# A two-layer adaptive feed-forward kernel: layer 1's order of instructions planned anew, layer 0's last sums regrouped, last outputs on two queues

## The chip, the cores and the metric

The kernel runs on one core of a Trainium2 chip. The core has a matrix engine (TensorE, PE in the profile; its weight loads are shown apart as PEld), a vector engine (VectorE, DVE), a scalar engine (ScalarE, ACT), GpSimd (POOL) and SyncE (SP), which here mostly issues DMAs. Each engine works through its own instructions in order, and semaphores make it wait for the others. The metric is the device time of one execution, in microseconds (us). Before the change the median of three runs was 423.62 us (423.48 to 424.63).

## The reference, cut to what matters

The input x has 8 batches of 128 tokens (1024 tokens) of 512 features. Each of two layers computes a condition from x, feeds it to a gated feed-forward network, and adds the result to x:

```python
# layer 0: base projection plus a gated mixture of 8 low-rank experts (top 2), then 4-bit weights
c = x @ W.T + 2.0 * sum_e gate[e] * (x @ A[e].T) @ B[e].T
x = x + (silu(c @ Wgate0) * (c @ Wup0)) @ Wdown0       # 1376 inner, weights dequantised by groups of 128

# layer 1: one 512x512 weight per batch, chosen by an index; RMS norm; then float32 weights
c = x @ weight[adapter_id].T
n = c * rsqrt(mean(c*c) + 1e-5) * ln_w
x = x + (silu(n @ gate_w.T) * (n @ up_w.T)) @ down_w.T  # 1792 inner
```

All of it is float32, and the result must be as exact as float32.

## The kernel before, in words

Activations are kept transposed: features on the 128 partitions (four chunks, `KC`), tokens along the free axis in two blocks `tb` of 512. `xT` is the residual x, updated in place and written out at the end.

**Splitting.** Most products are made with a faster matmul type. An operand is split into a high part (made on ScalarE, `high_of`, line 1069), a low part and a scaled difference (VectorE, `low_of` line 1072, `difference_of` line 1075). A sum takes high and low products ("H") and difference products ("D") into one PSUM bank, and between the two the bank is multiplied by a constant in place (`rescale`, done on ScalarE or VectorE through `scaled`, lines 1199 and 1201). TensorE therefore waits, at each change from H to D or back, for one engine to have gone over a bank.

**Layer 0** (`by_groups_of_scales`, the usual path) is written out by hand inside one `tc.manual_schedule` region: in it TensorE, VectorE and ScalarE issue in the order in which the code emits. Small splitting and dequantising jobs are put in queues for ScalarE and VectorE (`queue`), and are emitted when an estimate of the engines' load lets them (`spent` calls `pump`) or when `flush(name)` forces them out. The eleven chunks j of the inner dimension run in pairs (`gate_up_pair`, matmuls on line 659, `rescale` lines 299 and 301), and the down products (line 707) by blocks of chunks. The tail is `last_chunk_and_down`: gate and up of chunk 10 (96 wide), with the down products of chunks 8, 9 and 10 between them. `first(m)` multiplies chunk 8 into the sum of output chunk m, and needs the high part (first half of its matmuls) and the low part (second half, DVE line 313) of `h8`; `second(m)` adds chunk 9, after a rescale of the sum; last comes chunk 10, and `down_final` (line 719) adds the finished sum to `xT`. The last loop is over tb outside and m inside: all four m of the first 512 tokens, then all four of the other 512. Two of the four sums, m = 2 and 3, take the PSUM of `gate` and `up`, and so must wait until the silu (line 675) and the product h (line 678) have read these. Meanwhile `queue_first_weights` splits, for layer 1's chunk 0, two of four groups of weights: group 0 (high, low, difference, then sums of weights) and group 2.

**Layer 1** is not written by hand. `Plan` holds tasks, each with its engine or engines, an estimated duration, dependencies, a priority `key`, and the buffers it takes and gives. `Plan.run` plays them through at build time: of the tasks whose dependencies are done, the one with the lowest key begins on a free engine, and the instructions are emitted in that order (again inside a `manual_schedule` region of its own). A finished task is seen at once by tasks that can only run on the same engine, and by others after `SEEN[engine]` (0.22 us after PE, 0.16 us after ACT or DVE). Keys come from constants: `STEP`, `LEAD` (how far before a chunk its weights are split), `AT` (places of the 29 steps of a chunk), `DOWN_LAG`, `DOWN_LEAD`, `SOON` (how early the rows' norms come), `SOONER` and `FILL` (the first three chunks), `WAYS` (which rescales may go to either engine and which to ScalarE alone), and others.

The tasks: eight rows (batches, order `ROWS1`): `adapt` (float32 products with the batch's weight, line 1261, 8 matmuls a row), then square, root, reciprocal, nx, turn (transposes, line 1302), norm, and splits of the row's forms (lines 1226 to 1232). The first row reads the first 128 tokens of all four m of `xT`. Then 14 chunks: gate and up for a pair of token halves through seven products of combined operands (matmuls on line 1446, snapshots on 1480 and 1484, products h on 1534), 42 matmuls a chunk. The down products (line 1585) come in five blocks; a block's eight sums (tb, m) take H, a rescale, D, and then `done` (line 1624, VectorE) adds them to `xT`. In the last block each `done` also issues the DMA of that piece of `xT` to the output (line 1626), all nine on SyncE's queue; the last sum is done in two halves.

Of the kernel before, what the change touches and what calls it, by code (L numbers as in the profile page):

```python
# [14 lines left out]
F32 = mybir.dt.float32  # L15
# [8 lines left out]
P = 128  # L24
# [33 lines left out]
PASS = 0.2267  # L58
SEEN = {"pe": 0.22, "act": 0.16, "dve": 0.16, "pool": 6.0, "sp": 3.5}
ANY_ORDER = {"bank", "snap"}  # L60
LATE = {"snap": 6, "sl": 2, "h3": 4, "wd": 2, "d": 3}
STEP = 1.41
LEAD = 8.17
DOWN_LAG = 10.29
DOWN_LEAD = 12.73
SOON = 6.82
OWN = 7.12
MIXED = 0.75
X22_AT = 4.98
H_AT = 10.2  # L70
D_STEP = 5.98
R_AT = -7.84
DD_AT = 4.69
DONE_AT = 6.56
WAYS = [0, 0, 0, 0, 0, 1, 1, 1, 0, 0]
SOONER = [[10, 10, 10, 10], [30, 0, -1.09, 0], [40, 12.63, 0, 0]]
FILL = [2.15, 4.34, 16.57]
XS_ONLY = (0, 1, 2, 16, 17, 18)
WEIGHTS_AT = [0.55, 1.73, 1.0, 2.54]
AT = [0.0, -1.2, -2.2, 1.9, 0.51, 2.5, 2.78, 3.97, 3.64, 3.1, 4.78, 6.47, 5.56, 6.5, 7.0, 7.5, 1.66, 2.64, 5.26, 4.46, 3.66, 4.42, 4.78, 5.36, 8.09, 7.2, 6.62, 7.62, 8.03]  # L80
# [48 lines left out]
class Plan:  # L129
# [12 lines left out]
    def run(self):  # L142
# [10 lines left out]
        def begin(t, engine, us):  # L153
            nonlocal n
            waiting.remove(t)
            for k, who in t.takes:
                queue[k].remove(t)
                self.place[k, who] = self.slots[k].pop(0)
            t.on = engine
            if engine is not None:  # L160
                begun[engine] = now + us
                n += 1
                heapq.heappush(events, (now + us, n, None))
            own = [s for s in t.then if list(s.engines) == [engine]]
            for some, at in ((own, now + us), (None, now + us + SEEN.get(engine, 0.0))):
                n += 1
                heapq.heappush(events, (at, n, (t, some)))
            if t.fn is not None:
                t.fn(engine)
# [13 lines left out]
        while left:  # L183
# [5 lines left out]
            while events and events[0][0] <= now + 1e-6:  # L189
# [3 lines left out]
                t, some = t  # L193
                if some is None:
                    left -= 1
                    some = [s for s in t.then if list(s.engines) != [t.on]]
# [17 lines left out]
def network_in(ctx, tc, a, out, by_groups, flag, again):  # L214
# [25 lines left out]
    cp = cond_stack.enter_context(tc.tile_pool(name="cond", bufs=1, side="right"))  # L240

# [331 lines left out]
    def by_groups_of_scales():  # L573
# [129 lines left out]
        def down_product(ps, m, k, first, tbs=range(NTB)):  # L703
            n = CH0[k]
            for i in range(2):
# [9 lines left out]
            spent(2 * len(tbs))  # L715
# [19 lines left out]
        def last_chunk_and_down():  # L735
# [7 lines left out]
            def gate_up(c):  # L743
                for half, ps in enumerate(gu):
# [7 lines left out]
            def first(m):  # L752
                down_product(sums[m], m, j - 2, True)
                rescale(sums[m], ratio_d[:, m, j - 2 : j - 1])
# [7 lines left out]
            first(0)  # L762
            gate_up(1)
            first(1)
            gate_up(2)
            flush(f"h{j - 1}")
            second(0)
            gate_up(3)
# [13 lines left out]
            for tb in range(NTB):  # L782
                for m in range(KC):
                    down_product(sums[m], m, j, False, range(tb, tb + 1))
                    down_final(xT[:, m, tb * TB : (tb + 1) * TB], m, sums[m][:, tb], group)
# [31 lines left out]
        with tc.manual_schedule(engines={EngineType.PE, EngineType.DVE, EngineType.Activation}):  # L817

            nc.scalar.activation(root, eps, AF.Exp)
            exp0 = experts(0)  # L820
            x_high(0)
            x_low(0)
            x_scaled(0)
            exp1 = experts(1)
            for m in range(2):
                w_high(m)
            hg0 = gated(0, rows_of(exp0))
            for m in range(2, KC):
                w_high(m)
            kept = cp.tile([P, 2, 2 * (E + E * R)], F32, name="kept")  # L830
            nc.scalar.copy(kept, exp1[:, :, : 2 * (E + E * R)])
            x_high(1)
            scale_bT()
            pairs0, base0 = base_sums()
            for m in range(KC):
                base_products(base0, 0, m, 0)
            hgT0 = turned(hg0, exp0[:, 0, :])
            for m in range(KC):
                w_low(m)
                base_products(base0, 0, m, 1)  # L840
            x_low(1)
            x_scaled(1)
            for ps in pairs0:
                rescale_base(ps)
            pairs1, base1 = base_sums()
            for i in range(2):
                for m in range(KC):
                    base_products(base1, 1, m, i)
            x_diff(0)
            for m in range(KC):  # L850
                w_diff(m)
                base_products(base0, 0, m, 2)
            hg1 = gated(1, [kept[:, i].rearrange("p (b n) -> p b n", b=2) for i in range(2)])
            for ps in pairs1:
                rescale_base(ps)
            x_diff(1)
            queue_zeros(0, 4, "zeros")
            for j in range(4):
                queue_weights(j, f"w{j}")
            flush("w0")  # L860
            for i in range(2):
                for m in range(2 * i, 2 * i + 2):
                    low_rank(base0, hgT0, m)
                split_condition(0, pairs0[i], i)
            ratios(ratio, sc)
            flush("w1")
            ratios(ratio_d, scd)
            for m in range(2):
                base_products(base1, 1, m, 2)
            hgT1 = turned(hg1, base0[0])  # L870
            base_products(base1, 1, 2, 2)
            for i in range(2):
                for m in range(2 * i, 2 * i + 2):
                    if m == KC - 2:
                        base_products(base1, 1, KC - 1, 2)
                    low_rank(base1, hgT1, m)
                split_condition(1, pairs1[i], i)
                if i == 0:
                    for _ in range(2):
                        run("dve", 0)  # L880
            cond_stack.close()
            open_rw()
            pools["w1"] = w1_stack.enter_context(tc.tile_pool(name="w1", bufs=1, side="right"))
            hp = h_stack.enter_context(tc.tile_pool(name="h0", bufs=1, side="right"))
            load_down(*BLOCKS0[0])
            for pair0 in PAIRS0[2:4]:
                load_qw(*pair0)

            def dequantise(pair0, zeros=None):
                if zeros is not None:  # L890
                    queue_zeros(*zeros, "zeros")
                for j in range(*pair0):
                    queue_weights(j, f"w{j}")

            def ready(pair0):
                for j in range(*pair0):
                    flush(f"w{j}")

            load["act"], load["dve"] = clock[0] + 1.0, clock[0] + 2.0

            queue_down(*BLOCKS0[0], "d0", at=clock[0] + 7.0)
            gate_up_pair(0, 1)
            ready(PAIRS0[1])
            dequantise(PAIRS0[2], (4, 8))
            gate_up_pair(2, 3)
            flush("d0")
# [892 lines left out]
```

## Time and profile before

| | us |
|---|---|
| median of three runs | 423.62 |
| the profiled execution, its own time | 423.74 |
| its span, first to last instruction | 421.9 |
| PE busy | 411.8 |
| DVE busy | 373.0 |
| ACT busy | 307.0 |
| layer 0's last product starts / layer 1's first adapt product starts | 165.25 / 165.57 |
| last matmul ends | 415.28 |

The span is what the profile's views are about; 1.8 us of the execution's own time lie outside it. The mean granted TensorE clock is 0.995 over the span. In a timeline row the columns are: start, duration, engine, line, operation, output<-inputs, shape, how many were merged, and in brackets the idle time of that engine before it and who ended it. A matmul's duration contains its pipeline; what counts is the distance from one start to the next. In the chain of waits, 64 down products back to back (line 707, from 72.32 us) take 14.51 us, 0.2267 us each; ten adapt products (from 180.92 us) take 4.29 us, 0.429 us each; four transposes 0.44 us.

### The profile page before, as it was taken

How to read it: one execution, taken by the hardware profiler on the slowest of the kernel's cores; microseconds unless marked ns; L12 is line 12 of the kernel's file. 1: busy time of each engine (PE TensorE's matmuls, PEld its weight loads, DVE VectorE, ACT ScalarE, POOL GpSimd, SP SyncE). 2: the span in 40 equal slices, each digit the busy share in tenths (PEclk: the TensorE clock that was granted, in tenths of full speed). 3: DMA queues.
4: the chain of work that ended last, by engine and by line, in shares of the span. 5: the costliest groups of instructions: out<-in, count | busy, mean ns of one | idle time of the engine just before them, and what ended most of it. 6: DMA issues, size and time to landing. Idle time of an engine off the chain costs nothing.

```text
span 421.9 us, 5201 instructions
## 1 busy us (share of the span) xinstructions
PE 411.8 (98%) x1771; PEld 314.9 (75%) x1771; DVE 373.0 (88%) x678; ACT 307.0 (73%) x503; POOL 27.1 (6%) x34
## 2 busy tenths in 40 slices
PE   8999999999999999999999999999999999999993
PEld 8885778888888765445676777788778877887772
DVE  4799979997998689989999999988998899979963
ACT  5833798868796765668998787658975797669651
POOL 1000200000000300320011011011011001000000
PEclk9999999999999999999999999999999999999997
DMA  8931811010010720870163035033323134000014
GB/s 271 394 144 36 233 56 44 11 53 2 0 62 2 278 46 18 329 239 2 58 181 62 0 87 138 0 87 88 113 50 89 62 75 114 0 3 1 24 51 155
DMA packets 16913, 38.59 MB, mean 91 GB/s; under 512 B 1904, under 2 KB 8432, under 8 KB 15856
## 3 DMA queue, kind: packets, MB, share of 16 engines
q1 hardware_dynamic: 11344, 25.09, 17.8%
q0 software_dynamic: 4960, 12.06, 11.5%
q10 hardware_dynamic: 576, 1.05, 0.6%
q8 instruction: 15, 0.25, 0.2%
q14 instruction: 18, 0.15, 0.1%
HBM read 36.10 MB, written 2.10 MB: 91 GB/s over the span
## 4 chain that ended last, share of the span: by engine, by line
PE 85%; DVE 8%; ACT 4%; issue 1%; ACTq 0%; DVEq 0%
PE bank L1446 27%; PE bank L1585 17%; PE gate L659 9%; PE up L659 9%; PE down L707 8%; PE base L510 5%; PE bank L1261 5%; PE experts L413 2%; PE base L536 2%; DVE w L1072 1%; DVE xT L719 1%; DVE w L1075 1%; PE idle L366 1%; PE bank L1302 1%; DVE snap L1534 1%
## 5 line engine op out<-in xcount | busy, mean ns | idle before, releaser
L1199 ACT ACTIVATE bank<-bank 128x512 f32<-128x512 f32 x129 | 73.3, 584 | 31.9 <-PE bank L1446 17.6
L1585 PE MATMUL bank<-h,d 128*128 128x512 f32 x240 | 66.5, 391 | 0.2
L1585 PEld LDWEIGHTS bank<-h,d 128*128 128x128 f32 x240 | 44.8, 188 | 10.6 <-DVE snap L1480 0.6
L659 PE MATMUL gate<-a,dq 128*128 128x512 f32 (+1 forms) x176 | 47.8, 393 | 0.1
L659 PE MATMUL up<-a,dq 128*128 128x512 f32 (+1 forms) x176 | 47.4, 391 | 0.0
L1446 PE MATMUL bank<-xs,w 128*128 128x512 f32 x168 | 46.0, 396 | 0.8 <-ACT bank L1199 0.8
L1446 PE MATMUL bank<-a,w 128*128 128x512 f32 x168 | 45.2, 394 | 0.2 <-ACT snap L1199 0.2
L707 PE MATMUL down<-h,wd 128*128 128x512 f32 (+1 forms) x176 | 42.6, 395 | 0.6 <-DVE h L313 0.4
L707 PEld LDWEIGHTS down<-h,wd 128*128 128x128 f32 (+1 forms) x176 | 32.4, 188 | 10.0 <-DVE xT L719 1.3
L659 PEld LDWEIGHTS gate<-a,dq 128*128 128x128 f32 (+1 forms) x176 | 32.5, 185 | 8.5 <-ACT sl L675 0.6
L659 PEld LDWEIGHTS up<-a,dq 128*128 128x128 f32 (+1 forms) x176 | 32.4, 185 | 7.9 <-DVE a L791 0.4
L1446 PEld LDWEIGHTS bank<-xs,w 128*128 128x128 f32 x168 | 31.1, 188 | 9.1 <-ACT bank L1199 1.6
L1446 PEld LDWEIGHTS bank<-a,w 128*128 128x128 f32 x168 | 30.7, 188 | 9.0 <-ACT snap L1199 2.2
L1075 DVE SCALAR_TENSOR_TENSOR w<-w 128x512 fp32r<-128x512 f32 x50 | 34.5, 690 | 2.1
L299 ACT ACTIVATE gate<-gate,ratio 128x1024 f32<-128x1024 f32 (+1 forms) x24 | 26.1, 1086 | 10.7 <-PE gate L659 10.7
L1480 DVE SCALAR_TENSOR_TENSOR snap<-bank,snap 128x512 f32<-128x512 f32 x42 | 28.6, 684 | 4.9 <-ACT wz L1069 4.8
L1072 DVE TENSOR_TENSOR w<-raw,w 128x512 fp32r<-128x512 f32 x42 | 28.7, 684 | 3.1 <-ACT w L1069 3.1
L1062 POOL DMA_DIRECT2D raw<-in_wgu x14 | 17.4, 1246 | 208.2 <-PE gate L659 45.6
L1624 DVE SCALAR_TENSOR_TENSOR xT<-bank,xT 128x512 f32<-128x512 f32 (+1 forms) x41 | 27.4, 672 | 3.0 <-PE bank L1585 2.6
L1585 PE MATMUL bank<-w,d 128*128 128x512 f32 x96 | 29.4, 391 | 0.0
L1261 PE MATMUL bank<-w,xT 128*128 128x512 f32 x64 | 29.2, 596 | 0.0
L1199 ACT ACTIVATE snap<-bank 128x512 f32<-128x512 f32 x41 | 24.2, 593 | 5.9 <-PE bank L1446 5.8
(169 smaller groups left out, 736.9 us busy)
## 6 DMA issues: line engine op xcount, KB each, us to landing
raw<-in_wgu SPq DMA_DIRECT2D x14, 640.0 KB, 4.0
raw<-in_wgu POOLq DMA_DIRECT2D x14, 256.0 KB, 4.4
wd<-in_wd SPq DMA_DIRECT2D x14, 256.0 KB, 2.7
qw<-in_qw_gu SPq DMA_DIRECT2D x5, 512.0 KB, 4.7
xT<-in_xT SPq DMA_DIRECT2D x2, 1024.0 KB, 12.2
out<-xT SPq DMA_DIRECT2D x7, 256.0 KB, 2.0
xb<-in_xb ACTq DMA_DIRECT2D x4, 256.0 KB, 5.2
xb<-in_xb SPq DMA_DIRECT2D x4, 256.0 KB, 5.2
```

The costliest lines, as they stand in the source:

```text
L299: nc.scalar.activation(ps, ps, AF.Copy, scale=by)
L510: nc.tensor.matmul(base[m], lhsT=wT3[i][:, m, c * P : (c + 1) * P], rhs=x_parts(tb)[i][:, c, :], start=(i == 0 and c == 0), stop=(i == 1 a ...
L659: nc.tensor.matmul(ps, lhsT=dqs[j][:, c, half, :], rhs=a3[i][:, c, tb * TB : (tb + 1) * TB], start=(c == 0 and i == 0), stop=(i == 1), ski ...
L707: nc.tensor.matmul(ps[:, tb], lhsT=wds[k][:n, m * P : (m + 1) * P], rhs=h2[k][i][:, tb], start=(first and i == 0), stop=(i == 1), skip_gro ...
L1072: nc.vector.tensor_tensor(lo, raw, hi.bitcast(F32), ALU.subtract)
L1075: nc.vector.scalar_tensor_tensor(di, lo.bitcast(F32), -1.0 / EPS, hi.bitcast(F32), ALU.mult, ALU.add)
L1199: nc.scalar.activation(out_, in_, AF.Copy, scale=by)
L1261: nc.tensor.matmul(of("bank", "ad", b), lhsT=xT[:, c, b * T : (b + 1) * T], rhs=of("w1", b)[:, c * D : (c + 1) * D], start=(c == 0), stop= ...
L1446: nc.tensor.matmul(ps, lhsT=w[:, i, n, c * P : (c + 1) * P], rhs=x[i][:, c0 + c], start=(first and i == which[0] and c == 0), stop=True, s ...
L1480: nc.vector.scalar_tensor_tensor(x, of("bank", j, bank_), by, x, ALU.mult, ALU.add)
L1585: nc.tensor.matmul(of("bank", *who), lhsT=of("d", j)[:, i, m * P : (m + 1) * P], rhs=h_tile(j, tb)[:, i], start=(i == 0 and j == j0), stop ...
L1624: nc.vector.scalar_tensor_tensor(x, of("bank", *who)[:, q * w : (q + 1) * w], -EPS, x, ALU.mult, ALU.add)
```

## The change

1. `Plan.run`: a finished task is now seen by waiting tasks that have `"pe"` among their engines `WEIGHTS` = 0.11 us later than by others (unless that task can only run on the same engine). The buffers it gives come free as before.
2. Most constants of layer 1's keys have new values, two of the `WAYS` (snapshot v to ScalarE alone, snapshot u3 to either), and the assumed times at which VectorE and ScalarE become free for layer 1 (2.6 and 0.0 us for 2.0 and 0.3).
3. Group 2 of layer 1's chunk 0 is no longer split by `queue_first_weights` at the end of layer 0, but by tasks of the plan, as the other chunks' groups are.
4. `last_chunk_and_down`: `first(0)` is cut in two: its high half comes before `gate_up(1)` and its low half after it; the split of chunk 9's h is forced out between them. `second(0)` and the last gate and up products are interleaved by halves.
5. The last loop of layer 0 goes by m: both token blocks of one m (four matmuls), then one `down_final` over 1024 columns; for the last m two of 512.
6. The two `manual_schedule` regions become one, closed after the plan has run.
7. In the last block, the DMAs of sum 6 and of the first half of sum 7 are issued by ScalarE, the others by SyncE as before.

```diff
+WEIGHTS = 0.11
-STEP = 1.41
-LEAD = 8.17
-DOWN_LAG = 10.29
-DOWN_LEAD = 12.73
-SOON = 6.82
+STEP = 1.36
+LEAD = 7.63
+DOWN_LAG = 13.45
+DOWN_LEAD = 13.99
+SOON = 8.12
...
-WAYS = [0, 0, 0, 0, 0, 1, 1, 1, 0, 0]
-SOONER = [[10, 10, 10, 10], [30, 0, -1.09, 0], [40, 12.63, 0, 0]]
-FILL = [2.15, 4.34, 16.57]
+WAYS = [0, 0, 0, 1, 0, 0, 1, 1, 0, 0]
+SOONER = [[10, 10, 10, 10], [30, 0.2, -1.09, 3.36], [47.42, 20.05, 7.42, 7.42]]
+FILL = [2.92, 7.12, 17.38]
...
-            own = [s for s in t.then if list(s.engines) == [engine]]
-            for some, at in ((own, now + us), (None, now + us + SEEN.get(engine, 0.0))):
+            some = {True: [], "pe": [], False: []}
+            for s in t.then:
+                some[True if list(s.engines) == [engine] else "pe" if "pe" in s.engines else False].append(s)
+            seen = now + us + SEEN.get(engine, 0.0)
+            for some, at, last in (
+                (some[True], now + us, False), (some[False], seen, True), (some["pe"], seen + WEIGHTS, False)
+            ):
...
             gate_up(0)
-            first(0)
+            first(0, range(1))
+            flush(f"h{j - 1}")
             gate_up(1)
+            first(0, range(1, 2))
             first(1)
             gate_up(2)
             flush(f"h{j - 1}")
-            second(0)
-            gate_up(3)
+            second(0, range(1))
+            gate_up(KC - 1, range(1))
+            second(0, range(1, NTB))
+            gate_up(KC - 1, range(1, 2))
             queue_split(f"h{j}", h, h2[j])
...
-            for tb in range(NTB):
-                for m in range(KC):
-                    down_product(sums[m], m, j, False, range(tb, tb + 1))
-                    down_final(xT[:, m, tb * TB : (tb + 1) * TB], m, sums[m][:, tb], group)
+            for m in range(KC):
+                down_product(sums[m], m, j, False)
+                if m < KC - 1:
+                    down_final(xT[:, m, :].rearrange("p (b t) -> p b t", b=2), m, sums[m], group)
+                else:
+                    for tb in range(NTB):
+                        down_final(xT[:, m, tb * TB : (tb + 1) * TB], m, sums[m][:, tb], group)
...
-    plan = Plan(slots, {"dve": 2.0, "act": 0.3})
+    plan = Plan(slots, {"dve": 2.6, "act": 0.0})
...
-            if j == 0 and g in (0, 2):
+            if j == 0 and g == 0:
...
-                        nc.sync.dma_start(out=out[m * P : (m + 1) * P, cols], in_=x)
+                        by = nc.scalar if i >= NTB * KC - 2 and q == 0 else nc.sync
+                        by.dma_start(out=out[m * P : (m + 1) * P, cols], in_=x)
```

## The prediction

> **What bounds the kernel now.** First the page's busy times, then the stretches of the layers one by one.
>
> ```profile
> PE 411.8 (98%) x1771; PEld 314.9 (75%) x1771; DVE 373.0 (88%) x678; ACT 307.0 (73%) x503; POOL 27.1 (6%) x34
> ...
> 142.00:165.60 23.60, 22.95 (x94) 15.53 (x92) 19.50 (x31) 18.07 (x23) 0.00 (x0) 1.00 0.32 101
> 165.60:182.00 16.40, 16.05 (x48) 7.43 (x48) 15.24 (x32) 7.51 (x19) 5.88 (x5) 1.00 0.74 246
> 182.00:196.00 14.00, 14.00 (x43) 6.62 (x42) 12.38 (x28) 11.01 (x28) 1.04 (x1) 1.00 0.41 152
> 196.00:206.00 10.00, 9.17 (x40) 6.42 (x41) 9.25 (x21) 9.35 (x24) 0.00 (x0) 1.00 0.01 2
> 206.00:236.00 30.00, 29.83 (x125) 22.14 (x124) 28.95 (x51) 26.90 (x54) 2.57 (x2) 1.00 0.40 106
> 236.00:266.00 30.00, 29.75 (x127) 23.02 (x126) 28.76 (x49) 23.16 (x44) 2.40 (x2) 1.00 0.33 79
> 298.00:402.00 104.00, 104.00 (x450) 82.78 (x449) 95.24 (x162) 79.31 (x150) 4.81 (x4) 1.00 0.21 54
> ```
>
> TensorE is the bound, but its busy time hides small waits, since a matmul's 0.39 us overlaps the next. The counts show them: at 0.2267 us a matmul, 206 to 236 has 125 x 0.2267 = 28.3 of 30 us (1.7 lost), 236 to 266 has 28.8 (1.2 lost), 298 to 402 has 102.0 of 104 (2.0 lost). In 196 to 206, counted by kind (0.2267, adapt 0.429, transpose 0.11), some 8.3 of 10 us (1.7 lost), and from 165.6 to 196 about 0.8. So layer 1 loses 7.4 us, most of it in its first hundred; in 196 to 206 ScalarE (9.35 of 10) and VectorE (9.25) are nearly full.
>
> Where single waits lie, from the timeline:
>
> ```profile
> 147.66 0.73 PE L707 MATMUL down<-h,wd 128*128 128x512 f32 x2 [0.43 <-DVE h L313]
> ...
> 157.48 2.12 PEld L707 LDWEIGHTS down<-h,wd 128*128 128x128 f32 x10 [0.62 <-DVE h L678]
> ...
> 162.14 5.36 DVE L719 SCALAR_TENSOR_TENSOR xT<-down,small,xT 128x512 f32<-128x512 f32 x8
> ...
> 164.91 0.30 PEld L707 LDWEIGHTS down<-h,wd 96*128 96x128 f32 x2 [0.36 <-DVE xT L719]
> 165.57 0.30 PEld L1261 LDWEIGHTS bank<-w,xT 128*128 128x128 f32 x2 [0.36 <-DVE xT L719]
> ...
> 172.20 0.66 PE L1302 MATMUL bank<-ident,nx 128*128 128x128 f32 x4 [0.35 <-ACT nx L1199]
> ...
> 205.62 1.20 PE L1446 MATMUL bank<-xs,w 128*128 128x512 f32 x4 [0.75 <-ACT bank L1199]
> 206.65 1.07 PE L1446 MATMUL bank<-a,w 128*128 128x512 f32 x4
> ```
>
> Four matmuls take 1.20 us after a wait and 1.07 without one: besides the wait, about 0.11 us goes on a weight load that nothing covers (start to start 0.34 instead of 0.227). The end, SyncE's issues and one of the landings:
>
> ```profile
> 413.96 2.12 DVE L1624 SCALAR_TENSOR_TENSOR xT<-bank,xT 128x512 f32<-128x512 f32 x4 [0.90 <-PE bank L1585]
> ...
> 415.36 1.17 SPq L1626 DMA_DIRECT2D out<-xT  x1
> ...
> 417.17 0.87 SPq L1626 DMA_DIRECT2D out<-xT  x1
> ...
> DMA to landing us min/median/max: 2.5/2.5/2.5
> ```
>
> VectorE is done at 416.08; the last transfer is issued 1.1 us later, as its queue is busy with the two before it (1.17 and 0.45 us for an issue that takes 0.33 when the queue is free), and lands at 419.7; 2.2 us of closing follow.
>
> **The change, part by part.**
>
> *Layer 0's tail, gate and up.* The wait before 147.66 is for the low half of `h8`. Cutting `first(0)` lets eight matmuls (1.8 us) go between: 0.6 of waiting and 0.1 of weight load go. Late next is `gate_up(1)`: it moves up to 147.05, its gate sum leaves ScalarE's rescale at 147.07 and its up sum at 148.07, where the matmuls arrive at about 147.96, so 0.3 comes back. Forcing out the split of `h9` puts VectorE's low part (1.2) ahead of the rescales; a rescale on ScalarE from 149.05 (when the high part ends there) takes 1.1 and meets `gate_up(2)` at 150.4; behind the low part on VectorE it would end at 151.6 and cost 1.2. Net -0.3, bounds -0.7 to +0.8. The halving of the last gate and up ends the gate sum 0.45 sooner, so the silu (1.1) and h (1.27) that free the PSUM for `first(3)` end sooner by at most that; the wait before 157.48 falls from 0.5 to some 0.3: -0.2 (0 to -0.45).
>
> *Sums by chunk.* TensorE starts chunk 10's sixteen down matmuls at 161.09 and adapt at 165.57: 4.48 us, against 16 x 0.2267 = 3.63. The rest is that the second token block's product of each m waits for the first's `down_final` (0.67 us each, eight in 5.36). With four matmuls a sum nothing reads a sum still being made: -0.85. What it costs: VectorE's first addition starts after four matmuls, not two, at about 162.2 (without group 2's low part, 0.69 us, which stood in front of it at 161.53), and from 1.2 us each (the 1024-wide rows of VectorE) sums 0 to 2 are in `xT` at 163.4, 164.65 and 165.9, sum 3's first half at 166.6. Row 0's adapt pairs, from 164.72 at 0.86 us each, need them at 164.72, 165.6, 166.4 and 167.3: covered, by 0.5 for the third. If that cover goes, each 0.1 beyond it costs 0.1. Bounds 0 to -0.95.
>
> *Group 2 of chunk 0* moves 0.63 us of ScalarE and 1.37 of VectorE from layer 0's end into layer 1; VectorE's 0.69 in front of the additions is off the path now, and ScalarE has an idle 5.1 us before its first square (169.31) to take it. I take 0; if it lands after 193, where ScalarE runs without a break to 205.6, it costs up to 2.0.
>
> *One region.* The order across the boundary shows no gap now (0.32 us from the last product to adapt, explained by VectorE). No instruction is added: 0, bounds -0.3 to +0.3.
>
> *Layer 1's order.* Every matmul is still there, 924 of them on lines 1446 and 1585; what can change is the 7.4 us lost. Two pieces have visible causes. Row 0's turn waited 0.5 beyond need since its reciprocal stood behind VectorE's splits until 171.26 (root ready 170.32); larger `SOON` puts rows' norms ahead. And each wait behind a rescale pays the 0.11 that the planner had not counted; some 25 places in layer 1 do, 2.8 us. A planner that counts it prefers a task already loaded. I take a third of the loss, -2.4, since 196 to 266 is as much bound by ScalarE and VectorE as by order; bounds -5.0 (the stretch before 266 as dense as 298 to 402) and +2.0 (as much again lost in the first hundred us as a third of what is lost).
>
> [...]
>
> *The outputs.* ScalarE is idle from 413.86. Sum 6 is issued there at 415.36, its first half of 7 after it; SyncE is free at 415.0 and can issue the last half at 416.1 instead of 417.17. Landing after 2.5 gives 418.6; after 3.6 (the longest among these) 419.7, no gain. I take -0.8, bounds 0 to -1.1.
>
> [...]
>
> Sum: 423.74 - 0.3 - 0.2 - 0.85 - 2.4 - 0.8 = 419.2; the profiled execution is 0.12 above the median, so **419.1**.
>
> **Rivals.** (a) The new order loses as much as the old: VectorE has only 0.75 to 1.2 us idle in each of the three stretches from 196 to 266, and TensorE that arrives 1.35 earlier finds the same busy engines. For it: the full 196 to 206; against: ScalarE's idle 9 us in 165.6 to 182. Then 423.62 - 1.35 - 0.8 = 421.5, or, if the earlier start is also lost there, 422.8. (b) Slower: the splits moved into layer 1 and the chunk-2 splits that `SOONER` calls 7.4 us earlier stand on VectorE and ScalarE ahead of the rows' forms, so that chunk 0's first sums come late. Price: 2.0 for group 2 and three more splits' high and low (3 x 1.3 = 3.9) at worst, with the 1.35 of layer 0 lost as well: 423.62 - 0.8 + 2.0 to 5.9, or 424.8 to 428.7. It decides when more than 0.8 us of such work stands ahead between 193 and 206. For it: ScalarE's unbroken run there; against: the early idle time. (c) The planner counts 0.11 on every hand-over, though most are hidden; if it so leaves gaps that a real TensorE doesn't, nothing is lost (the engine goes on when it can), so no price of its own.
>
> **How the numbers follow.** The forecast, with layer 1 better by 1 to 5 us: 0.55, its own range 416 to 421. Rival (a): 0.27, split evenly between 421.5 and about 422.8. Rival (b): 0.16. Better than 415.5: 0.02. A measurement of this kernel tells 0.3% (1.3 us, so 422.35 and 424.9) from no change. Faster: 0.55 + 0.02 + 0.15 = 0.72; same 0.13; slower 0.15. The range, 415.5 to 424.9, leaves out some 0.17.
>
> **What would show it.** Right: no wait on line 313 in the middle of the tail; line 719 with three 1024-wide additions; adapt 3.6 us after chunk 10's first down product; the first hundred us of layer 1 with more matmuls per stretch; the last issue within 0.2 us of VectorE's end. Wrong: adapt waiting for additions to `xT`, TensorE waiting for rescales longer between 190 and 206, or SyncE's last issue landing no sooner.

## The result and the profile after

The changed kernel takes 425.33 us (median of seven executions, 424.94 to 426.46) against 424.14 us for the kernel before beside it: a ratio of 1.0034, with a 95% interval of 1.0025 to 1.0044. It is slower by about 1.4 us. One execution of all those below, in the run without the forced split of `h9`, was slow throughout (691.3 us at a mean granted clock of 0.559) and is left out there. The prediction had 419.1 with a range up to 424.9, so it missed in size and in sign.

The two profiled executions (span 421.9 before, 423.3 after) are first cut at three events that both have. "Lost" is the time from the first adapt product to the start of layer 1's last matmul, less 240.27 us: the work between them at the pitches given above (0.2267, 0.429 and 0.11 us, and 0.025 for two very short ones).

| stage, us | before | after | difference | predicted |
|---|---|---|---|---|
| start to the first gate product of layer 0 | 41.88 | 42.69 | +0.81 | 0 |
| from there to the first adapt product | 123.69 | 123.42 | -0.27 | -1.35 |
| from there to the start of the last matmul | 249.32 | 250.65 | +1.33 | -2.4 |
| of that, lost | 9.05 | 10.39 | +1.33 | |
| from there to the end of the span | 7.05 | 6.55 | -0.5 | -0.8 |

The first row is not the change: the instructions there are the same, and over the fourteen profiles of this study that start lay anywhere between 41.6 and 42.8, always 29.7 us after TensorE's first product. What moves that first product (11.9 to 13.1) was not followed. The page's busy times hide all of it, as they did before:

```profile
PE 409.2 (97%) x1771; PEld 316.7 (75%) x1771; DVE 374.4 (88%) x677; ACT 306.8 (72%) x504; POOL 27.6 (7%) x34
```

The stretches (columns: window, length, then busy time and number of instructions of PE, PEld, DVE, ACT and POOL, granted clock, DMA share, GB/s) show where layer 1 won and lost:

```profile
165.60:182.00 16.40, 16.40 (x51) 7.85 (x51) 16.02 (x33) 8.87 (x24) 5.95 (x5) 1.00 0.78 264
196.00:206.00 10.00, 9.86 (x44) 7.33 (x45) 9.24 (x21) 9.38 (x25) 0.00 (x0) 1.00 0.18 54
206.00:236.00 30.00, 26.10 (x113) 20.28 (x112) 27.48 (x49) 24.55 (x49) 2.53 (x2) 1.00 0.31 80
236.00:266.00 30.00, 29.12 (x125) 22.70 (x124) 29.34 (x51) 22.56 (x43) 2.42 (x2) 1.00 0.33 79
```

Up to 206 TensorE does more than before in the same time (51 matmuls against 48, then 44 against 40). Counted by work done, the loss after 40 us of layer 1's work is 1.30, where it was 2.95. But part of that lead is only a later wait: the kernel before has its 0.75 us at 205.62 behind it, and the changed kernel's waits of the same kind end at 208.65 and 209.54. After 45 us of work the losses are 2.57 and 3.36, a lead of 0.8.

```profile
208.65 0.73 PE L1461 MATMUL bank<-xs,w 128*128 128x512 f32 x2 [0.53 <-ACT bank L1214]
```

Then 206 to 236 has 113 matmuls against 125: twelve fewer, 2.7 us. Most of this is one place, where 3.36 us are lost before 224.46. The chain of waits, cut to 205 to 226, goes through it:

```profile
215.34 0.61 DVE d L1575
215.95 0.02 issue
215.97 6.30 DMA wd<-in_wd
222.29 0.63 ACT d L1568
222.91 0.49 ACT sl L1499
223.40 0.52 ACT w L1089
223.92 0.49 ACT bank L1214
```

And the timeline around it (rows of SyncE, ScalarE and TensorE):

```profile
215.36 0.33 SPq L1079 DMA_DIRECT2D raw<-in_wgu  x1
215.97 0.33 SPq L1563 DMA_DIRECT2D wd<-in_wd  x1
...
220.19 1.07 PE L1461 MATMUL bank<-xt,wz 128*128 128x512 f32 x4
...
222.29 0.63 ACT L1568 ACTIVATE d<-wd 128x512 fp32r<-128x512 f32 x1 [3.58 <-DMA wd<-in_wd]
...
223.82 0.59 ACT L1214 ACTIVATE bank<-bank 128x512 f32<-128x512 f32 x1
...
224.46 1.19 PE L1461 MATMUL bank<-a,wz 128*128 128x512 f32 x4 [3.20 <-ACT bank L1214]
```

The reader is to see a queue in front of a queue. SyncE issues the load of chunk 2's down weights (256 KB) at 215.97, as soon as VectorE has freed one of its two buffers (line 1575), but 0.6 us behind the load of chunk 5's gate and up weights (640 KB). It lands after 6.3 us; this kernel's median for such a load is 2.7, and the planner counts on 0.1 + 3.5. ScalarE works in order, and its next instruction is the split of those weights: it stands still for 3.58 us with a silu, a weight split and a rescale of a bank behind it. TensorE needs that rescale. In the kernel before, the same load was issued at 215.34 with nothing freshly ahead of it (the big load came 3.25 us after it, at 218.59):

```profile
DMA to landing us min/median/max: 3.3/3.3/3.3
```

More than the landing differs, though. In the kernel before, ScalarE came to the split of these weights only 5.4 us after they had landed (at 218.65):

```profile
224.03 0.63 ACT L1553 ACTIVATE d<-wd 128x512 fp32r<-128x512 f32 x1
```

By these times a landing after 6.3 us would have held up nothing there. In the new order ScalarE is free for the split at 218.71, 2.7 us after the load's issue: there is no slack left, and ScalarE waits for all that the load takes beyond 2.7 us.

Layer 0 gave back part of its gain. The forced-out split of `h9` puts VectorE's low part (line 324) ahead of the gate's rescale (line 312), which `gate_up(2)` needs; its product loses 1.06 us start to start:

```profile
149.80 1.23 DVE L324 TENSOR_TENSOR h<-h,h 128x1024 fp32r<-128x1024 f32 x1 [1.47 <-ACT h L334]
...
150.94 1.28 DVE L312 TENSOR_SCALAR gate<-gate,ratio 96x1024 f32<-96x1024 f32 x1
...
152.28 0.93 PE L670 MATMUL gate<-a,dq 128*96 128x512 f32 x3 [0.90 <-DVE gate L312]
```

### The profile page after: what moved, and what is told of

Its sections match the earlier page's. It is cut to its first block, busy times and chain, and to the rows that moved or that the text cites. A ratio compares the mean times of both kernels' runs of the same rounds, so it can differ in the third digit from the quotient of the medians.

```text
span 423.3 us, 5190 instructions
## 1 busy us (share of the span) xinstructions
PE 409.2 (97%) x1771; PEld 316.7 (75%) x1771; DVE 374.4 (88%) x677; ACT 306.8 (72%) x504; POOL 27.6 (7%) x34
## 4 chain that ended last, share of the span: by engine, by line
PE 70%; DVE 18%; ACT 5%; DMA 3%; issue 1%; SPq 0%; DVEq 0%; ACTq 0%
PE bank L1461 17%; PE bank L1600 13%; PE gate L670 9%; PE down L718 9%; PE up L670 8%; PE bank L1276 6%; PE base L521 5%; DVE w L1092 3%; DVE w L1095 3%; DVE snap L1495 2%; PE base L547 2%; DVE xT L1639 2%; DMA xb<-in_xb 2%; DMA wd<-in_wd 1%; DVE snap L1549 1%
## 5 line engine op out<-in xcount | busy, mean ns | idle before, releaser
L1214 ACT ACTIVATE bank<-bank 128x512 f32<-128x512 f32 x126 | 70.6, 582 | 19.2 <-PE bank L1600 11.4
L1461 PE MATMUL bank<-xs,w 128*128 128x512 f32 x168 | 44.8, 395 | 0.9 <-ACT bank L1214 0.5
L718 PE MATMUL down<-h,wd 128*128 128x512 f32 (+1 forms) x176 | 41.7, 391 | 0.1
L1639 DVE SCALAR_TENSOR_TENSOR xT<-bank,xT 128x512 f32<-128x512 f32 (+1 forms) x41 | 26.5, 671 | 5.5 <-PE bank L1600 5.5
L1600 PE MATMUL bank<-w,d 128*128 128x512 f32 x96 | 29.7, 391 | 0.0
```

What stands on the lines that cost most here:

```text
L718: nc.tensor.matmul(ps[:, tb], lhsT=wds[k][:n, m * P : (m + 1) * P], rhs=h2[k][i][:, tb], start=(first and i == 0), stop=(i == 1), skip_gro ...
L1214: nc.scalar.activation(out_, in_, AF.Copy, scale=by)
L1461: nc.tensor.matmul(ps, lhsT=w[:, i, n, c * P : (c + 1) * P], rhs=x[i][:, c0 + c], start=(first and i == which[0] and c == 0), stop=True, s ...
L1600: nc.tensor.matmul(of("bank", *who), lhsT=of("d", j)[:, i, m * P : (m + 1) * P], rhs=h_tile(j, tb)[:, i], start=(i == 0 and j == j0), stop ...
L1639: nc.vector.scalar_tensor_tensor(x, of("bank", *who)[:, q * w : (q + 1) * w], -EPS, x, ALU.mult, ALU.add)
```

## The experiments

The theory (T1): the new order is good for layer 1 by itself, and the slowdown is one landing. The rival: the new order leaves ScalarE and VectorE too full, and the wait only happens to sit at a load. A second question was what the parts in layer 0 and the outputs are worth alone.

**The two loads exchanged, nothing else.** Only SyncE's order changes; TensorE, VectorE, ScalarE and GpSimd have the same instructions in the same order.

```diff
+    if by_groups:
+        behind(loads["raw", 5], loads["wd", 2])
```

> The kernel after, with one pair of loads on SyncE's queue exchanged: the weights of chunk 5 (640 KB), issued at 215.36 us in the profile after, now go behind the down weights of chunk 2 (256 KB), issued at 215.97. Every other engine's order is the same. Theory 1 (a transfer): TensorE's 3.4 us wait at 220.87 is there because that 256 KB load took 6.3 us instead of about 3.3 behind the 640 KB, and ScalarE, which runs in order, stood at its high part with TensorE's rescale behind it. Then the load lands at about 219.3, ScalarE waits 0.6 us or less, TensorE's wait falls under 0.8 us and the time is 425.3 - 2.8 = 422.5 (421.8 to 423.2). Theory 2 (rival (b) of the prediction, too much work on ScalarE and VectorE): the load is only what was noted last, the wait comes back on a rescale nearby, and the time stays at 424.5 or more.

Measured 422.89 us (422.51 to 424.25, ten executions), 0.998 of the kernel before (0.9969 to 0.9991). One exchange on one queue takes some 0.5%, 2.3 us, from the changed kernel and turns its sign. The load, issued at 215.21 and now first, landed in 4.3 us, still not 2.7, and a smaller wait stayed:

```profile
215.21 0.33 SPq L1565 DMA_DIRECT2D wd<-in_wd  x1
...
215.64 0.39 SPq L1081 DMA_DIRECT2D raw<-in_wgu  x1
...
219.58 0.63 ACT L1573 ACTIVATE d<-wd 128x512 fp32r<-128x512 f32 x1 [1.60 <-DMA wd<-in_wd]
...
221.75 0.96 PE L1463 MATMUL bank<-a,wz 128*128 128x512 f32 x3 [1.22 <-ACT bank L1216]
```

So T1's second half holds: with the same instructions on ScalarE and VectorE, the time follows the landing. Whether the new order is good by itself is asked further down.

**The forced split of `h9` taken out.**

```diff
             first(0, range(1))
-            flush(f"h{j - 1}")
             gate_up(1)
```

> The kernel after without the new forcing-out of chunk 9's split between first(0)'s halves; all else as after. Theory 1: the low part on VectorE (1.2 us) stood in front of the gate sum's rescale, and TensorE's 1.06 and 0.16 us before gate_up(2) and the last gate sum come from that; without it they go, time 425.3 - 1.0 = 424.3 (423.9 to 424.7). Rival: six rescales for two engines in that stretch are too many in any order, the wait only moves, gain under 0.3 us.

Measured 426.05 to 426.87 in three executions, 1.0058 (1.004 to 1.0076): not faster than the changed kernel, but slower. The rescale of the gate came at once, as expected, but the low part of `h9` now comes late for the low half of `second(0)`:

```profile
152.81 1.21 DVE L324 TENSOR_TENSOR h<-h,h 128x1024 fp32r<-128x1024 f32 x1
...
154.07 0.50 PE L718 MATMUL down<-h,wd 128*128 128x512 f32 x1 [1.50 <-DVE h L324]
```

From the first gate to the first adapt product it takes 123.83 us against 123.42: the wait had moved, and cost more. The rest of the slowdown lies in layer 1 and was a surprise: at the late load TensorE loses 6.1 us (counted by work done) where the changed kernel loses 3.5, though its idle time there is no longer than that kernel's (3.15 and 3.20 us). The last section shows why.

**Both edits.**

```diff
             first(0, range(1))
-            flush(f"h{j - 1}")
             gate_up(1)
...
+    if by_groups:
+        behind(loads["raw", 5], loads["wd", 2])
```

> The kernel after with both: loads exchanged and no forcing-out. If the two losses are separate, they add up: 425.3 - 2.8 - 1.0 = 421.5 (420.6 to 422.3), 0.6% faster than the kernel before. If layer 1 is bound by ScalarE and VectorE, TensorE that comes 1.0 us earlier finds them no further, and this is no better than the exchange alone (422.5).

Measured 422.98 us (422.27 to 425.57, nine executions), 0.9984 (0.9969 to 0.9999). That is the exchange alone; taking the flush out brings nothing (layer 0's stage took 123.92). The wait of `gate_up(2)` can't be had back by moving VectorE's low part: one of the two waits for the other.

**Sums by chunk and the two-queue outputs on the kernel before (parts 5 and 7).**

```diff
-            for tb in range(NTB):
-                for m in range(KC):
-                    down_product(sums[m], m, j, False, range(tb, tb + 1))
-                    down_final(xT[:, m, tb * TB : (tb + 1) * TB], m, sums[m][:, tb], group)
+            for m in range(KC):
+                down_product(sums[m], m, j, False)
+                if m < KC - 1:
+                    down_final(xT[:, m, :].rearrange("p (b t) -> p b t", b=2), m, sums[m], group)
+                else:
+                    for tb in range(NTB):
+                        down_final(xT[:, m, tb * TB : (tb + 1) * TB], m, sums[m][:, tb], group)
...
-                        nc.sync.dma_start(out=out[m * P : (m + 1) * P, cols], in_=x)
+                        by = nc.scalar if i >= NTB * KC - 2 and q == 0 else nc.sync
+                        by.dma_start(out=out[m * P : (m + 1) * P, cols], in_=x)
```

> The kernel before with only two parts of the change: layer 0's last sums by chunk, and the last outputs from two queues. The prediction gave them -0.85 and -0.8. Theory of the prediction: both carry to the end, 424.1 - 1.4 to 1.6, so 422.6 (422.2 to 423.0). Rival: layer 1's rows wait on ScalarE and VectorE, which are no earlier, and eat the 0.85; only the outputs' 0.5 (from the profile after, end of the last matmul to the end 6.16 instead of 6.66) is left: 423.6.

Measured 423.27 us (422.75 to 424.2, eleven executions), 0.9988 (0.9978 to 0.9998): some 0.5 us faster, between the two expectations. Layer 0's stage is 122.78 against 123.69: the 0.85 predicted for the sums is there, 0.91 (three profiles of the old layer 0 took 123.57 to 123.86, so some 0.2 of it may be scatter). But in this build group 2's splits still stand on VectorE ahead of the first addition to `xT`, and adapt waits for the additions:

```profile
161.81 1.29 DVE L1075 TENSOR_TENSOR w<-raw,w 128x512 fp32r<-128x512 f32 x2 [0.40 <-ACT w L1072]
163.03 0.68 DVE L1078 SCALAR_TENSOR_TENSOR w<-w 128x512 fp32r<-128x512 f32 x1
...
163.63 4.98 DVE L719 SCALAR_TENSOR_TENSOR xT<-down,small,xT 128x1024 f32<-128x1024 f32 x5
...
164.96 0.30 PEld L1264 LDWEIGHTS bank<-w,xT 128*128 128x128 f32 x2 [0.21 <-DVE xT L719]
165.01 3.45 PE L1264 MATMUL bank<-w,xT 128*128 128x512 f32 x6
...
166.15 0.30 PEld L1264 LDWEIGHTS bank<-w,xT 128*128 128x128 f32 x2 [0.89 <-DVE xT L719]
```

The first six adapt products lose about 0.7 us this way (3.45 us, where six without a wait take 5 x 0.429 + 0.59 = 2.74), and layer 1's loss rises from 9.05 to 9.33. Moving group 2 (part 3) is what keeps the gain of part 5 in the full change: there the first fourteen adapt products take 6.17 us, which is 13 x 0.429 + 0.59. The prediction gave part 3 a zero.

**The changed kernel without the late load.**

```diff
-            "wd", {"sp": 0.1}, lambda _: nc.sync.dma_start(out=of("wd", j), in_=a["wd1"][:, j, :]), [fd_open], k - 10.0,
+            "wd", {"sp": 0.1}, lambda _: j == 2 and by_groups or nc.sync.dma_start(out=of("wd", j), in_=a["wd1"][:, j, :]), [fd_open], k - 10.0,
```

> The kernel after without the load of chunk 2's down weights (the one that took 6.3 us): its two high parts and the rest read what chunk 0's left in that buffer, so chunk 2's down products are of the wrong weights; all orders on TensorE, VectorE, ScalarE and GpSimd are the same. Exchanging two loads took 2.4 us off the kernel after and left a wait of 1.4 for a load of 4.3 us. Theory 1 (the load is all there is to that wait): all 3.4 us go, 425.3 - 3.4 = 421.9 (421.4 to 422.4), and no wait over 0.3 us stands at that place. Theory 2: once the load is away, ScalarE's own backlog keeps at least 1 us there, 422.9 as with the exchange.

Measured 422.64 us (422.59 to 422.71, five executions), 0.9966 (0.9953 to 0.9978). ScalarE does the same split without waiting, and 0.22 us is what is left at TensorE:

```profile
218.83 0.62 ACT L1568 ACTIVATE d<-wd 128x512 fp32r<-128x512 f32 x1
...
221.69 1.19 PE L1461 MATMUL bank<-a,wz 128*128 128x512 f32 x4 [0.22 <-ACT bank L1214]
```

Layer 1's loss is 8.16. So the load costs 10.39 - 8.16 = 2.2 us net (so without it some 1.2 us of its 3.4 would be waited elsewhere), and the new order's own gain over the old is 9.05 - 8.16 = 0.9, not the 2.4 forecast. These are single profiles; three with one and the same order of layer 1, the loads exchanged, lose 8.05, 8.41 and 8.50. By the times of all executions the load costs 2.9 us (0.9966 against 1.0034): this profile also ends 0.65 us sooner after the last matmul, and some executions of the changed kernel have a lower mean clock as well (0.993 or 0.994 where others have 0.997), as the last section shows.

**The exchange, with gate and up as before (part 4 undone).**

```diff
-            first(0, range(1))
-            flush(f"h{j - 1}")
+            first(0)
             gate_up(1)
-            first(0, range(1, 2))
...
-            second(0, range(1))
-            gate_up(KC - 1, range(1))
-            second(0, range(1, NTB))
-            gate_up(KC - 1, range(1, 2))
+            second(0)
+            gate_up(KC - 1)
...
+    if by_groups:
+        behind(loads["raw", 5], loads["wd", 2])
```

> The kernel after with the two loads exchanged and with gate, up, first and second of layer 0's last chunk in the order of before (sums by chunk, one region and outputs as after). From the profiles, first gate product to first adapt takes 123.69 us before, 123.42 and 123.46 after and with the exchange, and 122.78 with sums by chunk alone, so the interleaving costs 0.65. Theory: 422.9 - 0.65 = 422.2 (421.8 to 422.6). Rival: layer 1 waits on its own engines and eats it: 422.9.

Measured 422.31 us (421.08 to 423.52, nine executions), 0.9957 (0.9943 to 0.9971). Layer 0's stage is 122.81 against the changed kernel's 123.42: the interleaving by halves costs 0.6 us, where the prediction had a gain of 0.5. With the 0.91 of the sums this closes layer 0's account: -0.91 + 0.61 = -0.30, and the two profiles differ by -0.27.

**The planner's 0.11 alone (part 1 on the kernel before, old constants).**

```diff
+WEIGHTS = 0.11
...
+            for some, at, last in (
+                (some[True], now + us, False), (some[False], seen, True), (some["pe"], seen + WEIGHTS, False)
+            ):
```

> The kernel before with WEIGHTS = 0.11 in the planner and nothing else, constants as before. If counting the hand-over is itself worth what the prediction said (some 25 exposed loads of 0.11, 2.8 us, a part of it), layer 1 loses 1 to 2 us less than the 9.1 of before and the time is 422.0 to 423.0. If the order's worth lies in where loads and full engines happen to meet, which the planner does not see, it goes either way by up to 3 us.

Measured 428.26 us (427.22 to 428.47, four executions), 1.0099 (1.0083 to 1.0114): outside everything expected. Layer 1 loses 13.04. Counting a true cost made the order worse, probably since the constants had been chosen with a planner that did not count it; new waits stand where there were none, such as

```profile
316.15 1.20 PE L1451 MATMUL bank<-xs,w 128*128 128x512 f32 x4 [1.23 <-DVE snap L1485]
```

**The 0.11 set to zero, with the new constants** (on the kernel of the exchange with the old gate and up).

```diff
-WEIGHTS = 0.11
+WEIGHTS = 0.0
```

> The kernel of loads exchanged and old gate and up order (422.3), with WEIGHTS = 0 in the planner and all new constants. The constants and the count belong together if this loses as the count alone on the old constants did (428.3, four more than before): 424 or more. If the new constants are simply better, with or without the count: 421.5 to 423.

Measured 424.93 us (424.49 to 426.17, ten executions), 1.0027 (1.0016 to 1.0037), with a loss of 11.03 in layer 1: 2.6 us slower than with the count (422.31). Parts 1 and 2 belong together: in layer 1 either without the other loses more than neither (13.04 and 11.03 against 9.05).

**Layer 1 alone (parts 1 to 3, with part 6).** Layer 0's gate, up and sums and the outputs are as before.

```diff
-            first(0, range(1))
-            flush(f"h{j - 1}")
+            first(0)
...
-                        by = nc.scalar if i >= NTB * KC - 2 and q == 0 else nc.sync
+                        by = nc.sync
```

> The change's layer 1 alone: the planner's count, all new constants and group 2 of chunk 0 in the plan; layer 0's tail and the outputs as before. Theory (the change lost its time in layer 1, at the one load): layer 1's lost time is the 9.1 of before plus 1.3, as in the profile after, so 424.1 + 1.3 = 425.4 (424.5 to 426.5), with a wait of 3 us or more for the load of chunk 2's down weights. Rival: the collision came from TensorE's earlier arrival out of layer 0, and without it the new order shows its 2 us gain: 422.0.

Measured 425.8 us (424.85 to 426.67, six executions), 1.0046 (1.0032 to 1.0061). The wait is there without parts 4, 5 and 7: the load was issued at 215.22, 0.6 us behind the big one, and took 6.36. So the slowdown belongs to the new order of layer 1 and to nothing around it.

**The outputs alone (part 7 on the kernel before).**

```diff
-                        nc.sync.dma_start(out=out[m * P : (m + 1) * P, cols], in_=x)
+                        by = nc.scalar if i >= NTB * KC - 2 and q == 0 else nc.sync
+                        by.dma_start(out=out[m * P : (m + 1) * P, cols], in_=x)
```

> The kernel before with the last outputs from two queues and nothing else. From the profiles, end of the last matmul to the end of the span is 6.66 us before and 6.16 after; but 6.07 in the run with WEIGHTS alone, which issues all on SyncE as before. If the two queues are worth the 0.5 to 0.8 that the prediction took: 423.4 (423.2 to 423.7). If the difference between these profiles is chance: 424.1, and the tail 6.1 to 6.7.

Measured 423.65 us (422.9 to 423.93, twelve executions), 0.9994 (0.9985 to 1.0002): a gain of 0.25 us whose interval still holds zero. The issues do move, but the landings lengthen (the last one from 2.5 to 3.1 us). In the changed kernel, where VectorE ends at 417.94, the last half is issued at 417.97:

```profile
417.23 1.15 ACTq L1642 DMA_DIRECT2D out<-xT  x2
```

```profile
L1642 ACTq DMA_DIRECT2D out<-xT x2: 362/550/737, 417.2 to 417.6; - x2
```

The second of ScalarE's two issues took 0.74 us where the first took 0.36. From VectorE's end to the last landing it is 3.31 us there and 3.11 with the outputs alone, against 3.64 before; the two other kernels with SyncE alone showed 3.05 and 3.65. 1.1 us of waiting issues went, and 0.3 and 0.5 of it arrived in these two profiles, less than such ends scatter.

**A planner that expects loads later.** Two kernels do without the exchange and let the planner count more than 3.5 us on a load, so that the consumer moves away from it. Gate and up are as before.

```diff
-SEEN = {"pe": 0.22, "act": 0.16, "dve": 0.16, "pool": 6.0, "sp": 3.5}
+SEEN = {"pe": 0.22, "act": 0.16, "dve": 0.16, "pool": 6.0, "sp": 6.5}
```

> As e6 without the exchange, and the planner told that a load from SyncE is seen after 6.5 us instead of 3.5 (the two loads that delayed TensorE took 6.3 and 4.3). It then puts other ScalarE work ahead of the high part that waits for the load. Theory (the planner's only fault there is the load's time): no wait of more than 0.3 us for that load, time at or below e6: 421.0 to 422.2. Rival: loads counted so late push everything that needs them back, other waits open, 422.5 to 424.

Measured 422.53 us (422.07 to 422.98, six executions), 0.9961 (0.9948 to 0.9974). No wait at the load, which itself moved (issued at 217.38, 3.05 us behind the big one, it landed in 2.8), but others elsewhere (0.87 us lost before 276.68): as good as the exchange, no better. With 5.0 for 6.5:

```diff
-SEEN = {"pe": 0.22, "act": 0.16, "dve": 0.16, "pool": 6.0, "sp": 3.5}
+SEEN = {"pe": 0.22, "act": 0.16, "dve": 0.16, "pool": 6.0, "sp": 5.0}
```

> The kernel after with the old gate and up order in layer 0 (no exchange), and the planner told that loads from SyncE are seen after 5.0 us instead of 3.5. With 6.5 it was 422.5: no wait at the load, but 1.4 us lost again by another at 275.6. A value between moves ScalarE's work less; the load that stands behind none takes 3.3 to 4.3. Expected 421.5 to 422.5, a wait under 0.5 at the load. If orders made by the planner differ by chance as much as their constants, anything from 421.5 to 425.

Measured 421.22 us (420.86 to 421.92, six executions), 0.9937 (0.9925 to 0.995). It beats both kernels, the one before by 2.6 us and the changed one by about 4. Its stretch from 206 to 236 has 122 matmuls (113 in the changed kernel), and 236 to 266 has 128:

```profile
206.00:236.00 30.00, 29.30 (x122) 21.94 (x121) 29.55 (x54) 25.93 (x50) 2.53 (x2) 1.00 0.31 80
236.00:266.00 30.00, 29.49 (x128) 23.29 (x127) 29.45 (x51) 22.18 (x42) 2.42 (x2) 1.00 0.31 79
```

The load is no faster, 5.7 us from 215.1, but nothing waits for it: a silu, a weight split, two rescales and a split of h now stand ahead of the split of the down weights, which begins 0.5 us after the landing, and TensorE goes on. The last of these rows:

```profile
220.20 0.63 ACT L1085 ACTIVATE h<-snap 128x512 fp32r<-128x512 f32 x1
220.30 0.76 PEld L1457 LDWEIGHTS bank<-a,wz 128*128 128x128 f32 x4 [0.34 <-ACT bank L1210]
220.30 2.26 PE L1457 MATMUL bank<-a,wz 128*128 128x512 f32 x8
...
220.73 0.58 ACT L1210 ACTIVATE bank<-bank 128x512 f32<-128x512 f32 x1
...
221.25 0.61 ACT L1564 ACTIVATE d<-wd 128x512 fp32r<-128x512 f32 x1
```

Layer 1's loss is 7.27, the least of all fourteen kernels. Not all of that is the wait: the changed kernel without the load still lost 8.16, so about 0.9 comes from an order that is better elsewhere; why 5.0 gives it and 6.5 does not was not looked into.

A third buffer for the down weights, which would have let the load start earlier, was not tried.

## Why the prediction was wrong

**"Layer 1's order ... -2.4, bounds -5.0 and +2.0"** is the step that failed; measured in the profiles +1.33. It has two faults. The working looked at the engines and at weight loads inside TensorE only; it never followed SyncE's queue. A new order of tasks also moves the loads, and each moved load has a new neighbour on its queue and a consumer in order on some engine. Before, 5.4 us of slack lay between the landing and ScalarE's split; in the changed kernel ScalarE reaches the split 2.7 us after the load's issue, where the planner counts on 3.6 us and the load took 6.3. That is +2.2 by the run without the load.

The other fault is size: the order's own gain is 0.9, and "a third of the loss" had no row behind it. Sorted by how far each distance from start to start exceeds its pitch, layer 1's losses are:

| lost in one place, us | before | before, with the count | new constants, loads exchanged, no count | these, with the count | changed | changed, without the load |
|---|---|---|---|---|---|---|
| 0.08 to 0.14 (places) | 3.6 (34) | 2.9 (27) | 3.7 (34) | 2.2 (21) | 2.2 (21) | 2.6 (25) |
| less | 1.9 | 1.3 | 2.1 | 0.9 | 0.9 | 1.1 |
| more | 3.6 | 8.9 | 5.2 | 4.9 | 7.3 | 4.4 |

The first row is the size of an uncovered weight load (0.11); the prediction put some 25 places where 34 are counted. The count did what the step expected of it: with the old constants and with the new it takes places away. All small losses together fell by 2.4 us from before to the changed kernel (that this is the figure forecast is chance, as that was a third of all losses). But the larger waits grew by 3.8, and by 0.9 even without the load. That they would stay as they were is what the step took for granted.

The two visible causes that the step named were right as far as they went. Row 0's turn no longer waits its 0.5 us, and the first stretch of work did begin denser (0.8 us ahead after 45 us of work, before the late load). And the 0.11 for an uncovered weight load was real: four matmuls take 1.19 us after the wait at 224.46 and 1.07 without one, and the weight load starts there as the wait ends. So it did at 205.62 in the profile before:

```profile
205.62 0.77 PEld L1446 LDWEIGHTS bank<-xs,w 128*128 128x128 f32 x4 [1.18 <-ACT bank L1199]
```

But the price of a hand-over is not the gain from telling a planner of it.

**"Net -0.3"** for the reorder of gate and up, and **"-0.2"** for the halves: together +0.6 measured. The working held the right case, the rescale behind the low part on VectorE at 1.2 us, but took the rescale on ScalarE as likelier. ScalarE was on the up sum (line 310, at 150.11), and the gate fell to VectorE.

**"-0.85"** for the sums by chunk: 0.91 measured in layer 0's stage, by the mechanism named. The cover for the additions (0.5 us for the third) held only because group 2 had left VectorE, so **"I take 0"** for group 2 was a price read too narrowly: the parts need each other. The **one region** was never run alone; no run shows a cost of it.

**"-0.8"** for the outputs: the mechanism was right and the size off. The last issue moved to 0.03 us after VectorE's end, as forecast, but longer landings took most of the gain back; 0.25 measured, in an interval that holds zero, and -0.5 to the end of the span in the two profiles. The end "landing after 3.6, no gain" was nearer.

**The rivals.** (b), slower, had the right sign and the wrong mechanism: chunk 0's first sums came no later. It priced work standing ahead of ScalarE's and VectorE's rows, and what stood ahead was a wait for a DMA. Its "unbroken run" of ScalarE from 193 was misread: that row of the trace has idle stretches of 0.45 us before 194.46 and 0.75 before 196.57. (a), the order losing as much as before, is close to what the order would have done without the load (0.9 gained). (c) was wrong in its "no price of its own": what the planner counts decides the order on three engines, and the run with the count alone paid 1.0%, 4.2 us.

## What to carry to other kernels

When an order of instructions is planned anew, list the loads too: for each load that moves, what is now ahead of it on its queue, when it lands, how much slack is left until its consumer's turn, and what stands behind that consumer on an engine that works in order. In a planner, put in the landing time of a load that has company (here 4.3 to 6.4 us, not 3.5), and try a few values, since the result is not monotone: 3.5, 5.0 and 6.5 gave 425.3 (some 0.6 of it from the changed gate and up), 421.2 and 422.5 us. A better cost model with constants fitted to the old one can be worse than either; change both and measure both.

## What the runs showed of the hardware

**One load landed after 2.8 to 6.4 us, by what stood next to it on its queue.** Chunk 2's 256 KB landed in 3.3 us with the 640 KB load on the same queue 3.25 us behind it (before), in 4.3 to 4.8 with it 0.4 us behind (three kernels with the exchange), in 5.7 with it 1.1 us ahead (the planner with 5.0) and in 6.3 to 6.4 with it 0.6 us ahead (the changed kernel, without the flush of `h9`, and layer 1 alone); with it 3.05 us ahead it took 2.8 (the planner with 6.5). GpSimd's accumulating load was issued 2.4 to 2.6 us earlier in all but the last (4.5), so it does not tell them apart; what it adds to all was not measured.

**A wait of some three microseconds cost TensorE half its clock in two of three profiles.** In the profile of the run without the flush of `h9`, TensorE is idle for 3.15 us at the late load (220.76 to 223.91). The granted clock (PEclk, the number behind the five engines' busy times) falls to half some 2 us into that wait and is back 6.8 us later:

```profile
222.40:222.80 0.40, 0.00 (x0) 0.00 (x0) 0.00 (x0) 0.40 (x2) 0.40 (x1) 0.95 0.00 0
222.80:223.20 0.40, 0.00 (x0) 0.00 (x0) 0.31 (x1) 0.40 (x2) 0.26 (x1) 0.50 0.00 0
...
226.00:226.40 0.40, 0.40 (x2) 0.31 (x2) 0.40 (x2) 0.40 (x1) 0.00 (x0) 0.50 0.00 0
...
229.20:229.60 0.40, 0.40 (x2) 0.33 (x1) 0.00 (x0) 0.16 (x1) 0.00 (x0) 0.52 0.00 0
229.60:230.00 0.40, 0.40 (x3) 0.34 (x2) 0.00 (x0) 0.40 (x2) 0.00 (x0) 1.00 0.00 0
```

For 5.7 us of this TensorE had work, so about 2.8 us went on top of the wait; that is why this run loses 6.1 us there and not 3.5. With layer 1 alone the profile shows the same for 3.4 us (223.4 to 226.8), after 3.21 us of idling, and a loss of 4.9. The profile of the changed kernel shows no such dip after 3.20 us of idling. But of its seven executions four have a mean clock of 0.993 or 0.994 over the span and three 0.997; 3.4 us at half in 423 lowers the mean by 0.004. The four take 425.31 to 426.46 us, the three 424.94 to 425.33. So it is likely, though only argued from the means, that the wait cost half of the changed kernel's executions another 0.7 us. The kernels in which this wait is 1.6 us or less show 0.995 or more in all but one execution of one kernel.

Waits of one length differ in this. The clock fell 2.0 us after TensorE went idle in the run without the flush (at 222.76) and 2.8 us after with layer 1 alone (at 223.38), and not within 3.20 us in the changed kernel's profile. Behind the last matmul it fell after 2.1 us in the profile before (at 417.33) and after 3.7 us in the changed kernel's (at 420.82). The stretches in the clock's records are, within 0.02 us, whole multiples of 3.413: at full clock 413.01 us before and 416.43 after (121 and 122 times), at half 6.82 without the flush and 3.41 with layer 1 alone. An estimate from these four profiles: if the clock changed only at such steps, a border at 222.85 (58 steps ahead of the fall at 420.82) would have cut the changed kernel's wait into 1.59 and 1.61 us, where the two waits that ended at half clock had 2.0 and 2.8 us of idling in one step. No run shows what sets the steps or how much idling it takes.
